# The second plain feed-forward and the unpacking of 4-bit weights, written out as one hand-ordered list

## The chip, the cores and the metric

The kernel runs on one core of one Trainium2 chip, as one program. Its time is the device time of that core in microseconds (us); a result is the median of several executions. The core has five engines with a queue of their own each: TensorE (PE) multiplies matrices, VectorE (DVE) and GpSimd (POOL) do elementwise work, ScalarE (ACT) applies functions such as ReLU, and SyncE (SP) issues transfers. Each engine works through its queue in order. They wait for each other by semaphores.

## The reference

The model has two layers, eight stages in all, over an input `x` of 2 x 1024 tokens with 256 channels in float32. Each stage adds its result to `x`, and each begins with a layer norm. In the order of the computation:

```
x = x + attention_a(layernorm(x))           # layer 0
x = x + ffn0(layernorm(x))
x = x + attention_b(layernorm(x))
x = x + ffn0(layernorm(x))                  # the stage that is changed
x = x + attention_d(layernorm(x))           # layer 1
x = x + ffn1(layernorm(x))
x = x + ttt(layernorm(x))
x = x + ffn1(layernorm(x))
```

Two pieces matter here. The plain feed-forward of layer 0 is

```
h1  = relu(x @ W1.T + b1)      # 256 -> 512
h2  = relu(h1 @ W2.T + b2)     # 512 -> 512
out = h2 @ W3.T + b3           # 512 -> 256
```

and is used twice with the same weights. The feed-forward of layer 1 has three weight matrices (gate, up, down) that come packed: two 4-bit codes to an integer, and one scale for each block of 32 values. A code's low three bits stand for one of 0, 0.5, 1, 1.5, 2, 3, 4, 6, and its fourth bit for the sign. The unpacking turns them into float32 once, ahead of layer 1.

## The kernel before, in words

`x` stays on the chip for the whole program, as 16 tiles of 128 tokens by 256 channels. The function `build` (L1911) runs the stages one after another: the first attention with the first plain feed-forward mixed in, the second attention, `ffn0`, then `dequantize` three times, and after that the stages of layer 1. The attention stages are recorded in an order written out by hand: `in_order` (L277) keeps the order of PE, DVE, ACT and POOL as the code issues it, while SP is left to the framework's scheduler. `ffn0` and `dequantize` are not: there the scheduler orders all engines by its own priorities, and so it mixes the two on its own.

`ffn0` (L637) first makes the layer norm of all 16 tiles, in two halves of eight (`layernorm_T`, L137). DVE takes the statistics (L146, L147), ACT a square root (L148), DVE normalizes (L154), PE turns each tile (L160), and ACT and DVE by turns copy the result out. Then, for each of four groups of 512 tokens, PE multiplies by W1 and W2 (both L654, with a ReLU on ACT at L658) and by W3 (L663). DVE adds the result to `x` (L668), and POOL adds the bias b3 (L669). A float32 product appears in the trace as two records.

`dequantize` (L1325) treats one packed matrix in eight parts of 256 columns, 24 parts in all. For each part SP issues one transfer of codes (L1335) and eight of scales (L1337). DVE makes the magnitude codes `m` and the sign bits `sg` with four masks (L1344, L1345) and the first term `a` (L1352). ACT makes the second term `c` (L1353) and the sign (L1354). POOL adds `c` to `a` (L1355), DVE adds `m` (L1356), POOL multiplies by the sign (L1357), and DVE multiplies by the scales into the weights (L1358). All the tiles of a part have two buffers.

The first plain feed-forward already exists in a second form, `ffn0_pieces` (L403): a list of 22 steps for 512 tokens, which the attention stages lay between their own steps. Its layer norm is by pairs of tiles: `layernorm_stats` (L187), then `layernorm_apply` (L199) with a root in nine small DVE instructions (`rsqrt`, L165) and the normalization on POOL (L205). In this form b3 is added to `x` right after the norm.

Of the kernel before, what the change touches and what calls it, by code (L numbers as in the profile page):

```python
# [39 lines left out]
def interleave_into(out, a, b):  # L40

    interleave([lambda x=x: out.append(x) for x in a], [lambda x=x: out.append(x) for x in b])


class Net:
# [354 lines left out]
            for _, step in mixed(after[2][-held:], chunks[3].outputs):  # L400
                step()

    def ffn0_pieces(self, work, bank, i, w1, w2, w3, b1, b2, b3):  # L403

        nc = self.nc
        f = type("ffn", (), {})()
        f.mv, f.xn = {}, {}

        def stats(p):
            f.mv[p] = self.layernorm_stats(work, (i + 2 * p, i + 2 * p + 1))  # L410

        def rows(p):
            tiles = (i + 2 * p, i + 2 * p + 1)
            f.xn[p] = self.layernorm_apply(work, tiles, f.mv[p], 1, "fxn")
            for tt in tiles:
                xs = self.x[:, tt, :]
                nc.gpsimd.tensor_tensor(xs, xs, b3, ALU.add)

        def turn(p):
            if p == 0:  # L420
                f.xT = work.tile([P, 2, 512], F32, tag="fx", name="fxT", bufs=1)
            pt = bank("ln_t").rearrange("p (k t) -> p k t", k=2)
            for j in range(2):
                for kc in range(2):
                    nc.tensor.transpose(
                        pt[:, kc, j * P : (j + 1) * P], f.xn[p][:, j, kc * P : (kc + 1) * P],
                        self.ident,
                    )
            nc.vector.tensor_scalar_mul(f.xT[:, :, 2 * p * P : 2 * (p + 1) * P], pt, -1.0)

        def hidden(m, part, src, w, bias, dst):
            n = w.shape[1]
            if part == 0:
                f.ph = bank("ph")
                if m == 0:
                    h = work.tile([P, 4, 512], F32, tag=dst, name=dst, bufs=1)
                    setattr(f, dst, h)
            for kc in range(2 * part, 2 * part + 2):
                nc.tensor.matmul(
                    f.ph, w[:, kc, m * P : (m + 1) * P], getattr(f, src)[:, kc],  # L440
                    start=(kc == 0), stop=(kc == n - 1),
                )
            if 2 * part + 2 == n:
                nc.vector.tensor_scalar(
                    getattr(f, dst)[:, m, :], f.ph, bias[:, m : m + 1], 0.0, ALU.add, ALU.max
                )
# [187 lines left out]

    def ffn0(self, w1, w2, w3, b1, b2, b3):  # L637
        nc, tc = self.nc, self.tc
        with ExitStack() as ctx:
            big = ctx.enter_context(tc.tile_pool(name="f_big", bufs=1))  # L640
            work = ctx.enter_context(tc.tile_pool(name="f_work", bufs=2))
            ps = ctx.enter_context(tc.tile_pool(name="f_ps", bufs=2, space=PSUM))
            xT = self.layernorm_T(big, work, ps)
            for c in range(4):
                cols = slice(c * 512, (c + 1) * 512)
                h1 = work.tile([P, 4, 512], F32, tag="h1", name="h1")
                h2 = work.tile([P, 4, 512], F32, tag="h2", name="h2")
                for src, at, n, w, bias, dst in (
                    (xT, cols, 2, w1, b1, h1), (h1, slice(0, 512), 4, w2, b2, h2),
                ):  # L650
                    for m in range(4):
                        ph = ps.tile([P, 512], F32, tag="ph", name="ph", bufs=3)
                        for kc in range(n):
                            nc.tensor.matmul(  # L654
                                ph, w[:, kc, m * P : (m + 1) * P], src[:, kc, at],
                                start=(kc == 0), stop=(kc == n - 1),
                            )
                        nc.scalar.activation(dst[:, m, :], ph, AF.Relu, bias=bias[:, m : m + 1])  # L658
                for j in range(4):
                    tt = 4 * c + j  # L660
                    po = ps.tile([P, C], F32, tag="po", name="po")
                    for kc in range(4):
                        nc.tensor.matmul(  # L663
                            po, h2[:, kc, j * P : (j + 1) * P], w3[:, kc, :],
                            start=(kc == 0), stop=(kc == 3),
                        )
                    xs = self.x[:, tt, :]
                    nc.vector.tensor_tensor(xs, xs, po, ALU.add)  # L668
                    nc.gpsimd.tensor_tensor(xs, xs, b3, ALU.add)  # L669

# [651 lines left out]

    def dequantize(self, pool, name, packed, scales):  # L1325


        nc, tc = self.nc, self.tc
        out = pool.tile([P, 2, 2048], F32, name=name)
        N = 256  # L1330
        with tc.tile_pool(name=f"{name}_dq", bufs=2, side="right") as work:
            for lo in range(0, 2048, N):
                pk = work.tile([P, N], I32, tag="pk", name="pk")
                sc = work.tile([P, N], F32, tag="sc", name="sc")
# [6 lines left out]
                m = work.tile([P, 2, N], I32, tag="m", name="m")  # L1341
                sg = work.tile([P, 2, N], I32, tag="sg", name="sg")
                for dst, mask in ((m, 7), (sg, 8)):
                    nc.vector.tensor_single_scalar(dst[:, 0, :], pk, mask, ALU.bitwise_and)  # L1344
                    nc.vector.tensor_scalar(  # L1345
                        dst[:, 1, :], pk, 4, mask, ALU.logical_shift_right, ALU.bitwise_and
                    )

                a = work.tile([P, 2, N], F32, tag="a", name="a")
                c = work.tile([P, 2, N], F32, tag="c", name="c")  # L1350
                sign = work.tile([P, 2, N], F32, tag="sign", name="sign")
                nc.vector.tensor_scalar(a, m, 4.0, 0.0, ALU.subtract, ALU.max)  # L1352
                nc.scalar.activation(c, m, AF.Relu, bias=self.minus12, scale=2.0)  # L1353
                nc.scalar.activation(sign, sg, AF.Copy, bias=1.0, scale=-0.25)  # L1354
                nc.gpsimd.tensor_tensor(a, a, c, ALU.add)  # L1355
                nc.vector.tensor_tensor(a, a, m, ALU.add)  # L1356
                nc.gpsimd.tensor_tensor(a, a, sign, ALU.mult)  # L1357
                nc.vector.scalar_tensor_tensor(  # L1358
                    out[:, :, lo : lo + N], a, 0.5,
                    sc.unsqueeze(1).to_broadcast([P, 2, N]), ALU.mult, ALU.mult,  # L1360
                )
        return out

    def ffn1_parts(self, ps, work, i, deq):

# [545 lines left out]
def build(tc, ins, out, first=0, last=5):  # L1911
    nc = tc.nc
    with ExitStack() as ctx:
# [12 lines left out]
        with tc.tile_pool(name="w0", bufs=1) as w0:  # L1926
# [14 lines left out]
            for s in todo:  # L1941
                if s == "attn_a":
                    net.attn_a_ffn0(wa, wao, *rope_a, (w1, w2, w3, b1, b2, b3))
                elif s == "ffn0":
                    net.ffn0(w1, w2, w3, b1, b2, b3)
                elif s == "attn_b":
                    net.attn_b(wb, wbo, *rope_b, (w1, w2, w3, b1, b2, b3))
            if {"attn_d", "ttt"} & set(todo):
                w4 = ctx.enter_context(tc.tile_pool(name="w4", bufs=1, side="right"))
                deq = [  # L1950
                    net.dequantize(w4, k, ins[f"L1_ffn_{k}_packed"], ins[f"L1_ffn_{k}_scales"])
                    for k in ("gate", "up", "down")
                ]
        if "attn_d" in todo:
            net.attn_d_ffn1(wd, wdo, *rope_d, nlam, rms_w, deq)
        if "ttt" in todo:
# [103 lines left out]
```

## Time and profile before

The executions took 3041.03 us as the median of three (3031.7 to 3042.51). The profiled execution took 3038.91 us, and its records span 3037.2 us.

| stretch or engine | us |
|---|---|
| span of the profiled execution | 3037.2 |
| PE busy in the span | 2585.5 (85%) |
| DVE busy | 1953.5 (64%) |
| ACT busy | 1324.4 (44%) |
| POOL busy | 1039.6 (34%) |
| last matmul of the second attention ends | 882.0 |
| first statistics of the third attention start | 1041.8 |

Times inside the span count from its start. In rows of the trace, a name such as L654 is the line of the kernel; `h<-ph,b` says that the instruction writes `h` and reads `ph` and `b`; and a note such as `[1.44 <-POOL a L1357]` says how long the engine had been idle before and what ended that. The granted clock is the share of its full rate that TensorE was given.

### The profile page before, as it was taken

How to read it: one execution, taken by the hardware profiler on the slowest of the kernel's cores; microseconds unless marked ns; L12 is line 12 of the kernel's file. 1: busy time of each engine (PE TensorE's matmuls, PEld its weight loads, DVE VectorE, ACT ScalarE, POOL GpSimd, SP SyncE). 2: the span in 40 equal slices, each digit the busy share in tenths (PEclk: the TensorE clock that was granted, in tenths of full speed). 3: DMA queues.
4: the chain of work that ended last, by engine and by line, in shares of the span. 5: the costliest groups of instructions: out<-in, count | busy, mean ns of one | idle time of the engine just before them, and what ended most of it. 6: DMA issues, size and time to landing. Idle time of an engine off the chain costs nothing.

```text
span 3037.2 us, 66929 instructions
## 1 busy us (share of the span) xinstructions
PE 2585.5 (85%) x26384; PEld 1608.0 (53%) x26384; DVE 1953.5 (64%) x6736; ACT 1324.4 (44%) x2672; POOL 1039.6 (34%) x1672
## 2 busy tenths in 40 slices
PE   6999998999988757887878878878777988898988
PEld 2333344434434434565655555555555767677777
DVE  5777665766664456667776858678656656566552
ACT  2776840454453256465564556656622112112110
POOL 3445232212114466566665646556500000000000
PEclk8999997999999867898989888898988889999999
DMA  3000000000001000000000000000001101101100
GB/s 115 1 1 1 1 1 1 1 1 1 1 17 40 28 1 1 1 1 1 1 1 1 1 1 1 1 1 1 18 17 24 24 20 20 23 11 36 24 9 14
DMA packets 61979, 35.39 MB, mean 12 GB/s; under 512 B 43216, under 2 KB 58080, under 8 KB 61664
## 3 DMA queue, kind: packets, MB, share of 16 engines
q1 hardware_dynamic: 59472, 29.49, 3.7%
q8 instruction: 208, 3.41, 0.4%
q10 hardware_dynamic: 2192, 1.61, 0.2%
q14 instruction: 107, 0.88, 0.1%
HBM read 22.68 MB, written 8.39 MB: 10 GB/s over the span
## 4 chain that ended last, share of the span: by engine, by line
PE 38%; DVE 13%; ACT 7%; issue 4%; POOL 3%; DMA 0%; POOLq 0%; ACTq 0%; DVEq 0%
PE ph L1387 6%; PE po L1894 5%; PE pg L1881 4%; ACT p L1200 4%; PE e L1178 4%; DVE p L1189 4%; PE pu L1881 4%; PE dT L1237 3%; PE po L1404 2%; DVE p L1226 2%; POOL p L1213 1%; PE py L1254 1%; PE pq L1564 1%; PE kh L1564 1%; PE pa L1564 1%
## 5 line engine op out<-in xcount | busy, mean ns | idle before, releaser
L1189 DVE CUSTOM_DVE_ANT_0 p<-e,mask 128x512 f32<-128x512 f32 (+3 forms) x768 | 381.6, 553 | 108.9 <-PE e L1178 107.7
L1200 ACT ACTIVATE p<-p,nm 128x128 f32<-128x128 f32 (+7 forms) x512 | 389.9, 764 | 97.4 <-DVE nm L1189 88.1
L1213 POOL TENSOR_SCALAR p<-p,ra,neg_lam 128x128 f32<-128x128 f32 (+7 forms) x256 | 221.8, 866 | 238.1 <-DVE ra L1209 178.6
L1237 PE MATMUL dT<-ident,p 128*128 128x128 f32 x1152 | 198.7, 306 | 114.4 <-ACT pT L1241 32.0
L1241 ACT ACTIVATE pT<-dT 128x128 f32<-128x128 f32 (+7 forms) x256 | 165.4, 646 | 283.5 <-PE dT L1237 282.2
L196 POOL TENSOR_SCALAR ln_mv<-ln_mv 128x2 f32<-128x2 f32 x56 | 17.6, 315 | 730.0 <-DVE ln_mv L194 720.0
L1178 PE MATMUL e<-kT,qT 32*128 32x512 f32 (+3 forms) x1536 | 235.4, 628 | 28.4 <-DVE nm L1189 27.0
L1226 DVE CUSTOM_DVE_ANT_0 p<-p,rs 128x128 f32<-128x128 f32 (+7 forms) x256 | 207.7, 832 | 70.1 <-POOL p L1217 69.8
L1237 PEld LDWEIGHTS dT<-ident,p 128*128 128x128 f32 x1152 | 153.5, 157 | 173.6 <-POOL p L1217 51.4
L845 ACT ACTIVATE pr<-s 128x512 f32<-128x512 f32 (+3 forms) x384 | 157.3, 497 | 162.9 <-PE s L840 154.2
L1230 POOL TENSOR_SCALAR p<-p,md 128x128 f32<-128x128 f32 (+7 forms) x256 | 208.8, 816 | 25.4
L550 ACT ACTIVATE pr<-s 128x1024 f32<-128x1024 f32 (+1 forms) x192 | 145.3, 812 | 131.3 <-PE s L544 83.7
L1894 PE MATMUL po<-down,inter 128*128 128x256 f32 x576 | 164.8, 451 | 3.4 <-issue 2.2
L805 PE MATMUL s<-kT,qT 32*128 32x512 f32 (+3 forms) x768 | 155.3, 518 | 3.8 <-DVE q_pad L813 1.9
L1881 PE MATMUL pg<-xT,gate 128*128 128x256 f32 x576 | 151.5, 409 | 6.5 <-ACT xT L225 5.5
L555 ACT ACTIVATE pr<-pr 128x1024 f32<-128x1024 f32 (+1 forms) x192 | 152.1, 852 | 0.0
L813 DVE CUSTOM_DVE_ANT_0 masked<-s,mask 128x128 f32<-128x128 f32 (+3 forms) x256 | 110.6, 487 | 58.9 <-PE s L805 58.8
L1894 PEld LDWEIGHTS po<-down,inter 128*128 128x128 f32 x576 | 129.8, 230 | 27.8 <-issue 2.3
L558 POOL TENSOR_SCALAR_AFFINE_SELECT pr<-pr 128x256 f32<-128x256 f32 x128 | 90.1, 721 | 154.7 <-ACT pr L555 57.7
L1881 PE MATMUL pu<-xT,up 128*128 128x256 f32 x576 | 139.3, 386 | 0.0
L1887 DVE TENSOR_TENSOR inter<-inter,pu 128x512 f32<-128x512 f32 x72 | 49.3, 685 | 133.9 <-PE pu L1881 133.9
L1387 PE MATMUL ph<-xT,gate 128*128 128x256 f32 x448 | 121.0, 417 | 10.3 <-ACT xT L225 10.1
(313 smaller groups left out, 5398.4 us busy)
## 6 DMA issues: line engine op xcount, KB each, us to landing
uk_d<-uk SPq DMA_DIRECT2D x128, 32.0 KB, 1.9
r<-uk_d SPq DMA_DIRECT2D x8, 512.0 KB, 3.9
x<-in_L_attn_a_X SPq DMA_DIRECT2D x4, 512.0 KB, 6.1
qh_d<-qh SPq DMA_DIRECT2D x8, 256.0 KB, 2.6
o<-qh_d SPq DMA_DIRECT2D x128, 16.0 KB, 1.7
out<-x SPq DMA_DIRECT2D x4, 512.0 KB, 3.1
w<-in_L_ffn_W2T SPq DMA_DIRECT2D x1, 1024.0 KB, 7.8
pk<-in_L_ffn_gate_packed SPq DMA_DIRECT2D x8, 128.0 KB, 2.4
```

The lines of the kernel that those rows point to most:

```text
L845: nc.scalar.activation(pr[:, g, off:512], tiles[g][:, 0:m], AF.Exp, scale=0.25)
L1178: nc.tensor.matmul(own.tiles[h][:, a, 0 : hi - lo], made["q"][r : r + 32, a, t, :], kT[r : r + 32, a, lo:hi], start=True, stop=True,)
L1189: nc.vector.tensor_tensor_reduce(own.p[h][a][:, lo:hi], own.tiles[h][:, a, 0 : hi - lo], neg_row[:, T - nk + lo : T - nk + hi], -1.0, 3e38 ...
L1200: nc.scalar.activation(own.p[h][a], own.p[h][a], AF.Exp, bias=own.nm[:, h, a : a + 1], scale=-1.0, accum_out=own.sm[:, h, a : a + 1],)
L1213: nc.gpsimd.tensor_scalar(p1, p1, own.ra[:, h : h + 1], nlam[:, head : head + 1], ALU.mult, ALU.mult)
L1226: nc.vector.tensor_tensor_reduce(p0, p0, p1, own.rs[:, h, 0:1], -3e38, ALU.add, ALU.max, md)
L1230: nc.gpsimd.tensor_scalar(p0, p0, md, 1.0, ALU.add, ALU.mult)
L1237: nc.tensor.transpose(dT[:, kb, :], own.p[h][0][:, kb * P : (kb + 1) * P], self.ident)
L1241: nc.scalar.activation(pT[:, 0 : qb + 1, :], dT[:, 0 : qb + 1, :], AF.Exp)
L1387: nc.tensor.matmul(ph[:, j, :], w[:, kc, m * P : (m + 1) * P], f.xT[:, kc, :], start=(kc == 0), stop=(kc == 1),)
L1881: nc.tensor.matmul(ph[:, j, :], m_[:, kc, m * P : (m + 1) * P], f.xT[:, kc, :], start=(kc == 0), stop=(kc == 1),)
L1894: nc.tensor.matmul(f.po[:, b], inter[m // 2][:, m % 2, b * P : (b + 1) * P], wd[:, m % 2, (m // 2) * C : (m // 2 + 1) * C], start=(m == 0) ...
```

## The change

The changed kernel drops `ffn0` and replaces it by `ffn0_dequantize`. This makes the 22 steps of `ffn0_pieces` for each of four groups of 512 tokens, and lays the norm of the next group between the later steps of the present one. `dequantize` no longer issues its work; it returns four steps for each of the 24 parts: codes (the transfers), magnitudes (masks, `a`, `c`, sign, and POOL's first add), signs (DVE's add and POOL's multiply), and values (the product with the scales). The steps of neighbouring parts are staggered: in one round stand the values of part n-4, the signs of n-3, the magnitudes of n-2 and the codes of n. The two lists, 88 steps of products and norms and 96 steps of parts, are then laid between each other evenly, and the order on PE, DVE, ACT and POOL is kept as written. A new argument, `scalar`, puts the turned copy and the ReLUs of `ffn0_pieces` on ACT, as the old `ffn0` had its ReLUs, and gives its tiles a second buffer. The buffers of a part grow from two to between two and six. The products, the masks and the arithmetic are the same.

```diff
-            f.xn[p] = self.layernorm_apply(work, tiles, f.mv[p], 1, "fxn")
+            f.xn[p] = self.layernorm_apply(work, tiles, f.mv[p], 1 + scalar, "fxn")
...
-            nc.vector.tensor_scalar_mul(f.xT[:, :, 2 * p * P : 2 * (p + 1) * P], pt, -1.0)
+            xT = f.xT[:, :, 2 * p * P : 2 * (p + 1) * P]
+            if scalar:
+                nc.scalar.activation(xT, pt, AF.Copy, scale=-1.0)
...
+                if scalar:
+                    nc.scalar.activation(out, f.ph, AF.Relu, bias=bias[:, m : m + 1])
...
-    def ffn0(self, w1, w2, w3, b1, b2, b3):
+    def ffn0_dequantize(self, ffn, deq):
...
+            ps = ctx.enter_context(tc.tile_pool(name="f_ps", bufs=1, space=PSUM))
+
+            def bank(name):
+                return ps.tile([P, 512], F32, tag="g", name=name, bufs=8)
+
+            ctx.enter_context(self.in_order())
+            products = []
+            after = [
+                [step for _, step in self.ffn0_pieces(work, bank, 4 * n, *ffn, scalar=True)]
+                for n in range(4)
+            ]
+
+            products += after[0][:6]
+            for n in range(4):
+                products += after[n][6:12]
+                ahead = after[n + 1][:6] if n < 3 else []
+                interleave_into(products, after[n][12:], ahead)
+            unpack = []
+            for args in deq:
+                unpack += self.dequantize(work, *args)
+
+
+            parts = []
+            for n in range(len(unpack) + 4):
+                for m, lag in ((3, 4), (2, 3), (1, 2), (0, 0)):
+                    if 0 <= n - lag < len(unpack):
+                        parts.append(unpack[n - lag][m])
+            interleave(products, parts)
...
+            def codes():
+                pk, sc = tile_("pk", 4, N, dtype=I32), tile_("sc", 6, N)
...
+            def magnitudes():
+
+                pk = t["pk"]
+                m, sg = tile_("m", 3, 2, N, dtype=I32), tile_("sg", 2, 2, N, dtype=I32)
+                a, c, sign = tile_("a", 4, 2, N), tile_("c", 2, 2, N), tile_("sign", 3, 2, N)
...
+            def signs():
+                a = t["a"]
+                nc.vector.tensor_tensor(a, a, t["m"], ALU.add)
+                nc.gpsimd.tensor_tensor(a, a, t["sign"], ALU.mult)
...
+            return codes, magnitudes, signs, values
```

More of the change, by code (lines that the diff above doesn't have):

```diff
@@ L401, in attn_a_ffn0, with ffn0_pieces @@
                 step()
-    def ffn0_pieces(self, work, bank, i, w1, w2, w3, b1, b2, b3):
+    def ffn0_pieces(self, work, bank, i, w1, w2, w3, b1, b2, b3, scalar=False):
         nc = self.nc
@@ L420, in turn @@
             if p == 0:
-                f.xT = work.tile([P, 2, 512], F32, tag="fx", name="fxT", bufs=1)
+                f.xT = work.tile([P, 2, 512], F32, tag="fx", name="fxT", bufs=1 + scalar)
             pt = bank("ln_t").rearrange("p (k t) -> p k t", k=2)
@@ L428, in turn @@
                     )
-            nc.vector.tensor_scalar_mul(f.xT[:, :, 2 * p * P : 2 * (p + 1) * P], pt, -1.0)
+            xT = f.xT[:, :, 2 * p * P : 2 * (p + 1) * P]
+            if scalar:
+                nc.scalar.activation(xT, pt, AF.Copy, scale=-1.0)
+            else:
+                nc.vector.tensor_scalar_mul(xT, pt, -1.0)
         def hidden(m, part, src, w, bias, dst):
@@ L435, in hidden @@
                 if m == 0:
-                    h = work.tile([P, 4, 512], F32, tag=dst, name=dst, bufs=1)
+                    h = work.tile([P, 4, 512], F32, tag=dst, name=dst, bufs=1 + scalar)
                     setattr(f, dst, h)
@@ L443, in hidden @@
             if 2 * part + 2 == n:
-                nc.vector.tensor_scalar(
-                    getattr(f, dst)[:, m, :], f.ph, bias[:, m : m + 1], 0.0, ALU.add, ALU.max
-                )
+                out = getattr(f, dst)[:, m, :]
+                if scalar:
+                    nc.scalar.activation(out, f.ph, AF.Relu, bias=bias[:, m : m + 1])
+                else:
+                    nc.vector.tensor_scalar(
+                        out, f.ph, bias[:, m : m + 1], 0.0, ALU.add, ALU.max
+                    )
         def output(j):
@@ L633, in attn_a_chunk @@
         return chunk
-    def ffn0(self, w1, w2, w3, b1, b2, b3):
+    def ffn0_dequantize(self, ffn, deq):
         nc, tc = self.nc, self.tc
         with ExitStack() as ctx:
-            big = ctx.enter_context(tc.tile_pool(name="f_big", bufs=1))
             work = ctx.enter_context(tc.tile_pool(name="f_work", bufs=2))
[L642 to L669, printed above, removed]
@@ L1321, in attn_d_out, with dequantize, part, tile_ @@
         return squares, root, normalize, project
-    def dequantize(self, pool, name, packed, scales):
-        nc, tc = self.nc, self.tc
-        out = pool.tile([P, 2, 2048], F32, name=name)
+    def dequantize(self, work, out, packed, scales):
+        nc = self.nc
         N = 256
[L1331 to L1334, printed above, removed]
+        def part(lo):
+            t = {}
+            def tile_(name, bufs, *shape, dtype=F32):
+                t[name] = work.tile([P, *shape], dtype, tag=name, name=name, bufs=bufs)
+                return t[name]
+            def codes():
+                pk, sc = tile_("pk", 4, N, dtype=I32), tile_("sc", 6, N)
                 nc.sync.dma_start(pk, packed[:, lo : lo + N])
@@ L1340, in dequantize @@
                     )
-                m = work.tile([P, 2, N], I32, tag="m", name="m")
-                sg = work.tile([P, 2, N], I32, tag="sg", name="sg")
+            def magnitudes():
+                pk = t["pk"]
+                m, sg = tile_("m", 3, 2, N, dtype=I32), tile_("sg", 2, 2, N, dtype=I32)
+                a, c, sign = tile_("a", 4, 2, N), tile_("c", 2, 2, N), tile_("sign", 3, 2, N)
                 for dst, mask in ((m, 7), (sg, 8)):
@@ L1347, in dequantize @@
                     )
-                a = work.tile([P, 2, N], F32, tag="a", name="a")
-                c = work.tile([P, 2, N], F32, tag="c", name="c")
-                sign = work.tile([P, 2, N], F32, tag="sign", name="sign")
                 nc.vector.tensor_scalar(a, m, 4.0, 0.0, ALU.subtract, ALU.max)
@@ L1355, in dequantize, with values @@
                 nc.gpsimd.tensor_tensor(a, a, c, ALU.add)
-                nc.vector.tensor_tensor(a, a, m, ALU.add)
-                nc.gpsimd.tensor_tensor(a, a, sign, ALU.mult)
+            def signs():
+                a = t["a"]
+                nc.vector.tensor_tensor(a, a, t["m"], ALU.add)
+                nc.gpsimd.tensor_tensor(a, a, t["sign"], ALU.mult)
+            def values():
                 nc.vector.scalar_tensor_tensor(
-                    out[:, :, lo : lo + N], a, 0.5,
-                    sc.unsqueeze(1).to_broadcast([P, 2, N]), ALU.mult, ALU.mult,
-                )
-        return out
+                    out[:, :, lo : lo + N], t["a"], 0.5,
+                    t["sc"].unsqueeze(1).to_broadcast([P, 2, N]), ALU.mult, ALU.mult,
+                )
+            return codes, magnitudes, signs, values
+        return [part(lo) for lo in range(0, 2048, N)]
     def ffn1_parts(self, ps, work, i, deq):
@@ L1944, in build @@
                 elif s == "ffn0":
-                    net.ffn0(w1, w2, w3, b1, b2, b3)
+                    w4 = ctx.enter_context(tc.tile_pool(name="w4", bufs=1, side="right"))
+                    names = ("gate", "up", "down")
+                    deq = [w4.tile([P, 2, 2048], F32, name=n) for n in names]
+                    net.ffn0_dequantize((w1, w2, w3, b1, b2, b3), [
+                        (w, ins[f"L1_ffn_{n}_packed"], ins[f"L1_ffn_{n}_scales"])
+                        for n, w in zip(names, deq)
+                    ])
                 elif s == "attn_b":
                     net.attn_b(wb, wbo, *rope_b, (w1, w2, w3, b1, b2, b3))
[L1948 to L1953, printed above, removed]
         if "attn_d" in todo:
```

## The prediction

> **What bounds the kernel now.** The page gives a span of 3037.2 us with TensorE (PE) busy 85%, but that is a mean over stages. The change touches one stage: from the last matmul of the second attention (L872, ends 878.72 + 3.29 = 882.01) to the first statistics of the third attention (L193 at 1041.76), 159.75 us. So I read that stretch alone. First its busy times and granted clock, in windows (columns: window, length, then busy us and instruction count of PE, weight loads, DVE, ACT, POOL, then clock, DMA share, GB/s).
>
> ```profile
> 940.00:950.00 10.00, 8.41 (x16) 3.67 (x17) 4.22 (x13) 4.89 (x8) 5.07 (x4) 0.83 0.20 59
> ...
> 1050.00:1060.00 10.00, 8.30 (x20) 4.48 (x19) 2.52 (x8) 1.41 (x3) 2.36 (x4) 0.50 0.00 0
> ```
>
> ```profile
> 882.00:1042.00 160.00, 128.55 (x353) 68.00 (x352) 89.55 (x239) 53.20 (x87) 72.89 (x66) 0.93 0.13 39
> ```
>
> No engine fills the 160 us. PE's 128.55 is not all work: the 192 recorded passes of L654 follow each other every 0.43 us (26 in 11.43) and the 128 of L663 every 0.215 us (6 in 1.46), so they need 82.6 + 27.5 us; with eight turns of about 0.65 us PE needs 115 us. DVE and POOL are busy 89.55 + 72.89 = 162 us together, which is the length of the stage. Then the list of waits, 904 to 1030 us, where the unpacking of weights (L1335 to L1358) and the products overlap (waiter, releaser, total us, times, longest):
>
> ```profile
> ACT c L1353 <- DVE m L1345: 76.3, 19, 5.9
> ...
> POOL a L1355 <- ACT c L1353: 35.8, 15, 4.6
> DVE a L1356 <- POOL a L1355: 29.7, 21, 1.8
> POOL a L1357 <- DVE a L1356: 16.9, 20, 0.9
> PEld ph L654 <- ACT h L658: 12.5, 7, 3.6
> ...
> PE po L663 <- ACT h L658: 8.7, 5, 4.7
> ```
>
> The engines hand one part of a weight round in a ring: DVE masks, ACT's c, POOL's add, DVE's add, POOL's multiply, DVE's product. Successive parts start 5.4 to 5.5 us apart (L1358 at 917.79, then 923.28). A ReLU (L658) stands in ACT's queue behind c, so PE waits for the ring too. At one place two parts overlap already:
>
> ```profile
> 905.92 0.69 DVE L1356 TENSOR_TENSOR a<-a,m 128x512 f32<-128x512 f32 x1 [0.57 <-POOL a L1355]
> ...
> 906.53 0.28 DVE L1344 TENSOR_SCALAR sg<-pk 128x256 int32<-128x256 int32 x1
> 906.73 0.29 DVE L1345 TENSOR_SCALAR sg<-pk 128x256 int32<-128x256 int32 x1
> 906.75 1.39 POOL L1357 TENSOR_TENSOR a<-a,sign 128x512 f32<-128x512 f32 x1 [0.87 <-DVE a L1356]
> ...
> 906.93 1.50 DVE L1352 TENSOR_SCALAR a<-m 128x512 f32<-128x512 int32 x1
> ...
> 908.35 0.68 DVE L1358 SCALAR_TENSOR_TENSOR gate<-a,sc 128x512 f32<-128x512 f32 x1
> 908.60 1.55 POOL L1355 TENSOR_TENSOR a<-a,c 128x512 f32<-128x512 f32 x1 [0.46 <-DVE a L1352]
> ...
> 910.18 0.69 DVE L1356 TENSOR_TENSOR a<-a,m 128x512 f32<-128x512 f32 x1 [1.16 <-POOL a L1355]
> ```
>
> The reader is to see the durations. L1352 alone takes 0.42; here, beside POOL's L1357, 1.50. POOL's L1355 alone takes 1.26; started during DVE's L1358 it takes 1.55. One excludes the other.
>
> **The change part by part.**
>
> *The ring is pipelined.* In the new list DVE runs, for each part k, the product of part k-2 (V), the add of k-1 (S), then masks and a of k (M); POOL multiplies k-1, then adds c for k. One period, from the start of S: masks at 0.61 and 0.81 (pitch 0.20); POOL's multiply is ready at 0.87 (0.69 + 0.18) and takes the lock at 0.95, ending at 2.21, the lock free at 2.08; masks three and four and a run 2.08 to 2.9; V's lock is 2.85 to 3.38; POOL's add, ready at 3.08, runs 3.38 to 4.65; the next S starts at 4.68. The stretch above is this period with two masks missing: 910.18 - 905.92 = 4.26, plus 2 x 0.20 is 4.66. So 4.68 us a part, against 5.48.
>
> Here a rule speaks against the change. The Trainium skill, "SBUF — State Buffer", section "Who interferes with whom", says that GpSimd and a DVE instruction with two SBUF inputs or in a 2-port mode share one port pair, held for the whole instruction. Whole instructions sum to 4 x 0.285 + 0.42 + 2 x 0.69 + 2 x 1.265 = 5.47 us a part: nothing gained. The rows say less: L1352 ended 0.29 after POOL instead of 0.42, so POOL let go about 0.13 before its recorded end, and L1358 held about 0.53 of its 0.68. I take 4.68, and keep 5.47 as a rival.
>
> *Norms.* Removed: L146 to L160 as one block ahead of everything (16 x 0.54 of L154 on DVE, the Sqrt and its table load of 1.28). Added: eight pairs; each has stats (about 1.05 us, hidden while DVE waits for POOL's add), a root of nine small DVE instructions (1.74 us alone, 3.59 at most beside POOL elsewhere in this trace), and on POOL two L205 (1.09 together) and two bias adds (1.40). POOL's four stand ahead of its next add or multiply, whose DVE and ACT successors wait. Walking the same period with them inserted gives 8.23 for the first pair (root and POOL work together add 3.55) and two periods of 12.9 instead of 9.36 for the second. I charge 3.5 us each, between 1.74 (POOL's share hidden) and 4.23 (root plus 2.49 of POOL, nothing hidden).
>
> *Start.* The first code DMA left at 878.80; in the built order it now also waits for the last L872, so 882.05: codes land 884.5 (2.4 to land) and the second part's 3.9 us later (0.37 + 8 x 0.44 of SP issue), 888.4. DVE's last add ends 882.5; stats and root 885.3; masks of part 0, alternating with POOL's four, 887.5; POOL's add 889.4; S of part 0 at 889.45; the second root with POOL's multiply 892.9; masks of part 1 894.6; POOL free 895.6, its add 896.9. S of part 1 starts at 897.0. PE's first product starts near 895.9; in the old trace half-fed products ran from 891.9 and had by 903.8 done what takes 6.9 us, so this is worth about 1 us, no more.
>
> *ACT.* It now turns all eight pairs (0.6 each, half were DVE's 0.68) and keeps the 32 ReLUs of 0.67: about 58 us, hidden beside 129. With nothing to hide it, 2.4 us.
>
> *SP.* 24 x 3.9 = 94 us, four and six buffers ahead of DVE: hidden. Were it exposed, a part would still cost only 3.9.
>
> *Banks and PE.* Between pieces PE must wait for the second root, queued on DVE behind an add that waits for PE's first output: about 3 us idle, then three outputs. PE has (128 - 115) us of slack, so I charge only the clock: the 940 window shows 0.83 after a 3.6 us wait, 1.7 us lost; half of that on the ring, 0.8 x 3 = 2.4 us.
>
> *End.* Last S at 897.0 + 22 x 4.68 + 6 x 3.5 + 2.4 = 1023.4; multiply and V behind it 2.9 us: 1026.3. The statistics follow directly; the old 0.83 us wait for a bias add goes. The exp table load at 1067.12 (1.28) goes too; L1200's first mean was ready at 1067.99, so 0.4. Gain: 1041.76 - 1026.3 + 0.4 = 15.9, say 16 us. All else stands in the same order.
>
> **Sum.** The profiled execution took 3038.91 us (span 3037.2), so 3023 for its like; against the median of 3041.03 that is 3025 us.
>
> **Rivals.**
>
> *PE becomes the bound:* 0.30 chance. If roots and norms hide in DVE's waits, the stage ends at 895.9 + 115 + 3 = 1014: 28 us gained, 3013. For it: PE's is the longest single sum. Against it: 908.60 and 906.93 above.
>
> *Whole-instruction locking:* 0.17. 22 x 5.47 ends the stage near 1044, so within a few us of before; 3038 to 3044. For it: the skill's rule and the 162 us of DVE and POOL together. Against: the 4.26 measured.
>
> *The clock falls:* 0.06. The row at 1050 has 0.50 with PE busy 8.30 of 10, and the Trainium skill, "TensorE: Matmul & The Clock Gate", section "What's actually happening", gives half rate after an idle window of about 3.4 us; the idle of 3 us between pieces is close. The row at 940 would make each 1.7 us. If instead a share h of the products runs at half rate, PE needs 115(1 + h): it passes the ring at h = 0.13, the old end at 0.27, and is 0.5% slower than before from 0.40 on; at h = 0.5 it ends at 1069, 3068 us.
>
> **How the numbers follow.** The likeliest, the pipelined ring under the lock, has 0.47, centre 3025, own range 3016 to 3034 (period 4.3 to 5.1 over 22 parts). About 0.5%, 15 us, is what can be told from no change: below 3026 is faster. That takes 0.24 of the 0.47 and all 0.30: 0.54; the rest and the locked case: 0.40; the clock: 0.06. The range reaches down past 3013 and up to 3040.
>
> **What would show it.** S to S (the add with m) 4.5 to 4.9 us apart in plain parts and about 8 with a root; DVE's a or masks at 1.2 to 1.5 us beside POOL; third-attention statistics near 1026; granted clock above 0.85 in the stage. It is wrong if periods stay at 5.4, or if PE runs without waits for ACT.

## The result, and the profile after

The changed kernel takes 3040.47 us (median of 20 runs, 3033.15 to 3056.76), the kernel before beside it 3035.89 (20 runs, 3028.07 to 3043.74). The ratio is 1.0013, with a 95% interval of 1.0003 to 1.0023: nothing gained, 4.6 us lost. The forecast of 3025 missed by 15, and by more in what it said of the change: it put 16 us off a median of three runs (3041.03) that twenty runs put 5 us lower, so 16 down was forecast and 4.6 up came, 20.6 apart. The profiled executions say the same of the one stage that changed. From the end of the last projection of the second attention (the last matmul of L881, before L872) to the third attention's statistics (L193) it was 882.01 to 1041.76, 159.75 us; it is 882.89 to 1046.65, 163.8 us. The forecast ended it at 1026.3.

To follow the rows after: masks L1362 and L1363, a L1366, ACT's c L1367 and sign L1368, POOL's add L1369, DVE's add L1373 (S), POOL's multiply L1374, DVE's product L1377 (V), ReLU L451, products of h1 and h2 L444, outputs L460, their add to x L465.

First the windows of the kernel after (window, length, busy us and count of PE, weight loads, DVE, ACT, POOL, then clock, DMA share, GB/s), for the two stretches shown of before:

```profile
882.00:1042.00 160.00, 127.57 (x347) 69.37 (x346) 111.94 (x286) 54.48 (x88) 92.90 (x87) 0.89 0.16 40
...
940.00:950.00 10.00, 10.00 (x25) 4.49 (x24) 6.25 (x15) 4.63 (x8) 4.04 (x3) 1.00 0.11 30
```

DVE and POOL are now busy 205 us in 160, against 162 before, so they do overlap. Some of the rise is time in which one stands locked out by the other (a mask of 0.28 us alone takes 1.36 beside POOL's multiply, rows below). PE fills the ten microseconds from 940 completely. It does so only in the h1 and h2 products; over the stage its clock is 0.89 against 0.93.

Then the waits of the kernel after, 904 to 1030 us (waiter, releaser, total us, times, longest), to lay beside those of before:

```profile
ACT h L451 <- PE ph L444: 35.1, 18, 4.3
ACT c L1367 <- DVE m L1363: 25.6, 9, 3.8
DVE a L1373 <- POOL a L1369: 23.7, 8, 5.4
POOL a L1369 <- ACT c L1367: 17.9, 5, 5.4
...
PE po L460 <- ACT h L451: 9.6, 3, 3.2
```

New at the top is ACT waiting for PE: 35 us in which the ReLU at the head of ACT's queue has no product yet. Below it POOL's add waits for c, and DVE's S for that add. Before, 76 us of ACT waiting for DVE's masks stood at the top.

The place where this happens, in order of time (start, us, engine, line, operation, tiles, idle time before it and its releaser):

```profile
939.46 0.68 DVE L1373 TENSOR_TENSOR a<-a,m 128x512 f32<-128x512 f32 x1
...
940.26 0.28 DVE L1363 TENSOR_SCALAR m<-pk 128x256 int32<-128x256 int32 x1
940.28 1.39 POOL L1374 TENSOR_TENSOR a<-a,sign 128x512 f32<-128x512 f32 x1 [1.29 <-DVE a L1373]
...
940.56 0.69 ACT L451 ACTIVATE h<-ph,b 128x512 f32<-128x512 f32 x1 [3.41 <-PE ph L444]
...
942.28 0.69 ACT L451 ACTIVATE h<-ph,b 128x512 f32<-128x512 f32 x1 [1.03 <-PE ph L444]
...
944.00 0.69 ACT L451 ACTIVATE h<-ph,b 128x512 f32<-128x512 f32 x1 [1.03 <-PE ph L444]
...
944.58 0.71 ACT L1367 ACTIVATE c<-m,minus 128x512 f32<-128x512 int32 x1
...
945.37 1.27 POOL L1369 TENSOR_TENSOR a<-a,c 128x512 f32<-128x512 f32 x1 [3.70 <-ACT c L1367]
...
946.67 0.69 DVE L1373 TENSOR_TENSOR a<-a,m 128x512 f32<-128x512 f32 x1 [3.72 <-POOL a L1369]
```

The second of the two masks that c needs is done at 940.54. In the list, c stands behind the third ReLU of h1. PE delivers one h1 product every 1.72 us, so ACT comes to c only at 944.58, four microseconds later. POOL's add and S wait for it: this period is 7.21 us. Nothing else held it, for a was ready at 942.35. The profile puts seven of POOL's waits in the stage down to c. This is one; the others are:

```profile
906.45 1.27 POOL L1369 TENSOR_TENSOR a<-a,c 128x512 f32<-128x512 f32 x1 [5.41 <-ACT c L1367]
983.82 1.28 POOL L1369 TENSOR_TENSOR a<-a,c 128x512 f32<-128x512 f32 x1 [2.98 <-ACT c L1367]
1023.51 1.28 POOL L1369 TENSOR_TENSOR a<-a,c 128x512 f32<-128x512 f32 x1 [4.23 <-ACT c L1367]
1028.66 1.27 POOL L1369 TENSOR_TENSOR a<-a,c 128x512 f32<-128x512 f32 x1 [1.62 <-ACT c L1367]
1035.53 1.27 POOL L1369 TENSOR_TENSOR a<-a,c 128x512 f32<-128x512 f32 x1 [3.33 <-ACT c L1367]
1041.03 1.27 POOL L1369 TENSOR_TENSOR a<-a,c 128x512 f32<-128x512 f32 x1 [2.10 <-ACT c L1367]
```

The one at 945.37 and the first three here are the same place of each of the four pieces, the h1 products. At the next two c stands behind ReLUs of the last piece's h2. These six are 21.3 us. At the last, 1041.03, c waits for its masks, which stand on DVE behind an output's add to x that PE has not served yet.

Three more waits, 4.9 us in all, are put down to DVE's statistics in the profile's list, but end like the others 0.08 us after a c that stands behind a ReLU without a product:

```profile
910.22 0.69 ACT L451 ACTIVATE h<-ph,b 128x512 f32<-128x512 f32 x1 [2.75 <-PE ph L444]
...
910.81 0.71 ACT L1367 ACTIVATE c<-m,minus 128x512 f32<-128x512 int32 x1
...
911.60 1.27 POOL L1369 TENSOR_TENSOR a<-a,c 128x512 f32<-128x512 f32 x1 [1.62 <-DVE ln_st L193]
```

Its masks were done at 908.84, and POOL's add does not read the statistics. So nine times, 26.1 us in all, POOL waited for a c behind ReLUs.

The other direction, at the end of the first piece's h2 products:

```profile
922.73 0.72 ACT L1367 ACTIVATE c<-m,minus 128x512 f32<-128x512 int32 x1 [3.80 <-DVE m L1363]
924.14 0.63 ACT L1368 ACTIVATE sign<-sg 128x512 f32<-128x512 int32 x1 [0.69 <-DVE sg L1363]
...
924.68 0.67 ACT L451 ACTIVATE h<-ph,b 128x512 f32<-128x512 f32 x1
...
925.40 5.84 PE L460 MATMUL po<-w,h 128*128 128x256 f32 x18 [3.18 <-ACT h L451]
```

The last product of h2 ends at 920.48 in the trace. Its ReLU stands behind c and sign of a part, which wait for DVE's masks, and these for POOL; it starts at 924.68. PE idles 3.2 us here, and then the first eight passes follow each other every 0.43 us instead of 0.22. So each of the two strands waits for the other in turn, through ACT's queue. I read from this that the stage comes to the slower of the two in each stretch, added up, which is more than either strand's own sum; the two strands by themselves, below, allow an estimate of it.

### The profile page after: what moved, and what is told of

Its sections match the earlier page's. It is cut to its first block, busy times and chain, and to the rows that moved or that the text cites. A ratio compares the mean times of both kernels' runs of the same rounds, so it can differ in the third digit from the quotient of the medians.

```text
span 3039.6 us, 66932 instructions
## 1 busy us (share of the span) xinstructions
PE 2582.3 (85%) x26384; PEld 1607.1 (53%) x26384; DVE 1977.6 (65%) x6786; ACT 1325.3 (44%) x2672; POOL 1062.2 (35%) x1696
## 4 chain that ended last, share of the span: by engine, by line
PE 59%; DVE 19%; ACT 8%; issue 5%; POOL 5%; DMA 0%; SPq 0%; POOLq 0%; DVEq 0%; ACTq 0%
PE ph L1409 5%; PE po L1916 5%; PE pg L1903 4%; DVE p L1198 4%; PE ph L444 4%; PE e L1187 4%; PE pu L1903 4%; ACT p L1209 4%; PE s L814 4%; PE dT L1246 3%; PE s L849 2%; PE py L868 2%; PE s L553 2%; POOL p L1222 2%; DVE p L1235 2%
## 5 line engine op out<-in xcount | busy, mean ns | idle before, releaser
L854 ACT ACTIVATE pr<-s 128x512 f32<-128x512 f32 (+3 forms) x384 | 157.3, 496 | 162.8 <-PE s L849 154.2
L1409 PE MATMUL ph<-xT,gate 128*128 128x256 f32 x448 | 119.8, 414 | 10.4 <-ACT xT L225 10.1
```

The lines of the kernel that those rows point to most:

```text
L1409: nc.tensor.matmul(ph[:, j, :], w[:, kc, m * P : (m + 1) * P], f.xT[:, kc, :], start=(kc == 0), stop=(kc == 1),)
```

## The experiments

Theory 1: the ring's pace and the norms are as the prediction had them; the list deals the steps by count, and ring and products stop each other through the in-order queues, ACT's first. Theory 2: the lock between DVE and POOL is the bound, and the ring alone is no faster. Theory 3: PE's own losses, half clock after each idle and the norms between pieces, are the bound. All stage lengths below are from one profile each, measured as above; against before, the stage moved by +4.0, -2.4, -10.1, -14.6 and -15.9 us in the five kernels that were also timed (the changed one, by time, add later, one root, one root by time), and the medians by +4.6, -0.3, -13.0, -17.5 and -21.3.

**The ring without products.** The list of steps stays, products are replaced by nothing; the feed-forward is not computed.

```diff
-            interleave(products, parts)
+            norms = [s for a in after for s in a[:6]]
+            interleave([s if s in norms else (lambda: None) for s in products], parts)
```

> The changed list with the products of the feed-forward left out (the matmuls of h1, h2 and the outputs, their ReLUs and the adds of the outputs to x), everything else at its place: so the feed-forward is not computed, while norms, turns and all unpacking run. Theory 1 (the ring's own pace under the lock is what the walk said, 4.68 us a part and 3.5 us for each pair of norms, and in the changed kernel it stands still behind the products, and they behind it): the adds with m start 4.5 to 4.9 us apart in plain parts, about 8.2 with a root, and from the second to the last of the 24 it is 115 to 128 us, against 144.3 in the changed kernel. Theory 2 (DVE and POOL are the bound: with whole instructions excluding each other the ring needs 5.47 us a part by itself): 140 us or more, plain parts 5.4 apart.

From the second S to the last it is 125.85 us, and the stage 144.7. In the changed kernel the same path is 144.29, from 898.81 to 1043.11. DVE's rows of this kernel (lines are one higher: S is L1374, masks L1363 and L1364, a L1367, V L1378):

```profile
898.99 0.69 DVE L1374 TENSOR_TENSOR a<-a,m 128x512 f32<-128x512 f32 x1 [2.96 <-POOL a L1370]
899.60 0.29 DVE L1363 TENSOR_SCALAR m<-pk 128x256 int32<-128x256 int32 x1
...
900.00 1.36 DVE L1363 TENSOR_SCALAR sg<-pk 128x256 int32<-128x256 int32 x1
...
901.82 0.68 DVE L1378 SCALAR_TENSOR_TENSOR gate<-a,sc 128x512 f32<-128x512 f32 x1
903.65 0.69 DVE L1374 TENSOR_TENSOR a<-a,m 128x512 f32<-128x512 f32 x1 [1.15 <-POOL a L1370]
...
1024.84 0.69 DVE L1374 TENSOR_TENSOR a<-a,m 128x512 f32<-128x512 f32 x1 [1.15 <-POOL a L1370]
```

The period is 4.66 us with the masks of one part beside POOL's multiply (1.36 instead of 0.28 for the one that is locked out), just as in the prediction, and the periods with the first root of a piece are 8.20. Theory 2 is out.

Set against the changed kernel part by part, the periods of the four h1 places above are 8.94 against 4.66, 7.21 against 4.65, 6.51 against 4.65 and 7.76 against 4.74. They make 11.7 of the 18.4 us between the two paths. The four periods that follow them, where c stands behind a ReLU of h2, add 2.9, and the last two of the path 3.8. The periods with adds of outputs to x add 2.5: these adds stand on DVE and are left out here. Against this, 2.45 us go the other way: one period of the ring alone is 8.70 and not 6.25, because set-up of the next stage (L975 to L995) comes to stand among POOL's work there (1000.81 to 1004.85). In the changed kernel this set-up comes after the last part.

**The products without the ring.**

```diff
-            interleave(products, parts)
+            for w, packed, _ in deq:
+                for half in range(2):
+                    nc.sync.dma_start(w[:, half, :], packed.bitcast(F32))
+            interleave(products, [])
```

> The changed list with the unpacking left out: the three weights are filled by plain loads of the packed codes, so their values are meaningless, while the feed-forward and its norms run as in the list. From the end of the last projection of the second attention to the third attention's statistics: theory 1 (each of the two, products and ring, is well below the sum of their waits on each other): 125 to 135 us (115 us of matmuls, about 8 ahead of the first one with norms of 4 us each and small stalls between pieces), against 163.7 in the changed kernel. Theory 3 (the clock's loss after each idle and the norms between pieces keep the products themselves from being faster): 145 us or more.

The stage is 126.5 us. PE's row of windows of this kernel:

```profile
878.00:1004.00 126.00, 118.12 (x352) 65.07 (x352) 27.89 (x121) 26.43 (x40) 21.23 (x42) 0.96 0.11 45
```

PE is busy 118 of 126 us at a clock of 0.96. Theory 3 is out: norms between pieces and the start cost PE little when no ring is in the way. So the two strands need 144.7 and 126.5 us by themselves, and 163.8 together.

An estimate for one piece, from the eighth S of the changed kernel (939.46) to the fourteenth (978.62): beside h1 and h2, PE's 48 passes at 0.43 us need 20.6, and the three parts there take 17.6 in the ring alone. Beside outputs and turns, the next three parts take 17.3 in the ring alone, and PE needs some 8 (32 passes at 0.215, two turns of 0.65). The slower in each stretch makes 20.6 + 17.3 = 37.9; measured are 39.2, of which 0.9 go to the adds to x. The ring's own sum is 34.9, PE's 29.

**Steps dealt out by time.**

```diff
-            interleave(products, parts)
+            pe = ring = 0.0
+            for k, step in enumerate(products):
+                step()
...
+                ring += 3.5 * (step in norms)
+                pe += 1.72 * (step in long)
+                while parts and ring + parts[0][0] / 2 <= 1.2 * pe:
+                    us, part = parts.pop(0)
+                    ring += us
+                    part()
```

> The same products in the same order and the same unpacking, but the steps of the unpacking are dealt out by time (1.72 us for each step of products, 4.7 for a part, 3.5 for each pair of norms) and not by count, so that more parts stand beside the h1 and h2 products and fewer beside outputs and norms. Theory 1: the adds with m inside h1 and h2 come about 4.7 apart, the waits of outputs for ReLUs and of ring for c become small, and the stage is 8 to 14 us shorter than in the changed kernel (150 to 156 us), the whole 3026 to 3033. Theory 2 (lock) and theory 3 (clock): within 3 us of the changed kernel.

The stage is 157.3 us, 6.4 shorter than in the changed kernel, a little less than expected; the whole is 3035.73, ratio to before 0.9998 (0.9986 to 1.0010). Thirteen of its periods are 4.66 to 4.68, as expected, but three are 11.3 to 11.7, which was not. Its waits, 904 to 1030 us:

```profile
PE ln_t L426 <- POOL ln_xn L205: 13.1, 7, 4.3
DVE x L465 <- PE po L460: 12.3, 3, 4.3
...
POOL a L1384 <- ACT c L1382: 8.6, 3, 3.9
```

Three waits for c are left. The other loop is through DVE, here at the first of the three long periods:

```profile
933.86 3.05 PE L460 MATMUL po<-w,h 128*128 128x256 f32 x8
...
936.95 0.42 DVE L465 TENSOR_TENSOR x<-x,po 128x256 f32<-128x256 f32 x1 [3.85 <-PE po L460]
937.29 0.69 DVE L1388 TENSOR_TENSOR a<-a,m 128x512 f32<-128x512 f32 x1
```

An output's add to x stands ahead of S on DVE, the output stands behind a turn on PE, the turn waits for POOL's normalized rows, and these for the root on DVE. This deal moved waits more than it removed them.

**POOL's add one part later.** M stays one step of the list, without POOL's add; that comes a part later, with one more buffer for each tile that lives longer. The dealing by count stays, but the list has 24 steps more, and against the products M comes to stand two or three steps earlier: that of the ninth part before the first h1 product of its piece, not behind the third (worked out from the two lists).

```diff
-                nc.gpsimd.tensor_tensor(a, a, c, ALU.add)
+            def adds():
+                nc.gpsimd.tensor_tensor(t["a"], t["a"], t["c"], ALU.add)
...
-            for n in range(len(unpack) + 4):
-                for m, lag in ((3, 4), (2, 3), (1, 2), (0, 0)):
+            for n in range(len(unpack) + 5):
+                for m, lag in ((4, 5), (3, 4), (1, 2), (2, 3), (0, 0)):
```

> POOL's addition of c is a step of its own, one part later in the list, with one more buffer for m, sg, a, c, sign and sc; nothing else. So a c that stands behind a ReLU has a whole period before anyone waits for it. Theory 1 in its narrow form (c late behind ReLUs holds the ring): the waits of POOL's add for c go from 17.9 us in sum to below 5, and the stage is 5 to 10 us shorter than in the changed kernel, after some 3 us for the longer drain. Theory 2 (lock) or theory 3 (clock): 0 to 4 us longer, by the drain.

The stage is 149.7 us, 14.1 shorter than in the changed kernel, more than expected, and the whole is 3023.06 (15 runs), ratio to before 0.9959 (0.9947 to 0.9970). Its waits, 904 to 1030 us (POOL's add is L1371, its multiply L1376):

```profile
POOL a L1376 <- DVE a L1375: 27.9, 15, 5.6
...
PEld ph L444 <- ACT h L451: 2.5, 5, 1.5
POOL a L1371 <- ACT c L1367: 1.9, 1, 1.9
```

POOL's waits for c fell from 17.9 us to 1.9, and those of the outputs on PE for a ReLU are gone. Is it the room or M's new place? At that h1 place c is not late any more, so the place has its share. But as in the changed kernel, c starts late (0.9 to 6.8 us after its masks) directly behind a ReLU in nine parts, in part the same and in part others, and only once does POOL wait. For example:

```profile
1016.23 0.28 DVE L1363 TENSOR_SCALAR m<-pk 128x256 int32<-128x256 int32 x1
...
1019.27 0.69 ACT L451 ACTIVATE h<-ph,b 128x512 f32<-128x512 f32 x1 [2.75 <-PE ph L444]
...
1019.86 0.71 ACT L1367 ACTIVATE c<-m,minus 128x512 f32<-128x512 int32 x1
...
1022.09 1.31 POOL L1371 TENSOR_TENSOR a<-a,c 128x512 f32<-128x512 f32 x1
```

This c is 3.35 us late, not much less than that of 944.58 in the changed kernel (4.04), and POOL's add needs it only 1.5 us after its end. The waits show the room at work; the 14.1 us are not split between the two. What POOL waits for now is DVE, which is busy 126.1 of the 151 us:

```profile
885.00:1036.00 151.00, 125.80 (x355) 68.38 (x354) 126.09 (x292) 54.15 (x88) 94.17 (x94) 0.91 0.17 42
```

**Control: the ring of that kernel without products** (the first experiment's edit on it; the feed-forward is not computed).

> The list with POOL's addition of c one part later, and the products of the feed-forward left out as before (matmuls of h1, h2 and outputs, ReLUs, the adds of outputs to x), so the feed-forward is not computed. Control for what the later addition does to the ring by itself. If the gain of 14 us with the later addition came from c no longer standing in the way: the ring by itself gains little, S of the second to S of the last part 121 to 126 us (125.8 with the addition in its old place), plain parts 4.5. If the later addition made the ring itself faster and the products never mattered: 110 to 115 us.

122.74 us from the second S to the last, plain parts 4.48, the stage 142.8. So the later add makes the ring itself only 3.1 us faster on that path (125.85 to 122.74), and takes 12.1 of the 18.4 us that the products had put on it: 144.29 less 125.85 is 18.4, 129.06 less 122.74 is 6.3. (Set-up of the next stage stands among POOL's work in this run too, and lengthens one period by 1.3 us, against 2.45 in the other; without it the later add takes 13.3 of 20.9.) Of the 6.3 nearly all lies in two periods, 8.27 against 6.12 and 8.29 against 4.49, where S stands on DVE behind an output's add to x that waits for PE, 1.71 and 3.39 us. The second:

```profile
1027.87 0.42 DVE L465 TENSOR_TENSOR x<-x,po 128x256 f32<-128x256 f32 x1 [3.39 <-PE po L460]
1028.21 0.68 DVE L1375 TENSOR_TENSOR a<-a,m 128x512 f32<-128x512 f32 x1
```

**The overlap undone.** M, S and V of a part follow each other in one round of the list, with products between them as before.

```diff
-                for m, lag in ((3, 4), (2, 3), (1, 2), (0, 0)):
+                for m, lag in ((1, 2), (2, 2), (3, 2), (0, 0)):
```

> The changed list with the ring's overlap undone: masks, the add with m, the multiplication and the product of one part follow each other in one step, as the kernel before handed a part round, while products, norms and the places of the steps stay. If the overlap works and its gain was given back by waits on the products: S of the second to S of the last part 150 to 170 us against 144.3 in the changed kernel, the stage 170 to 185. If the overlap never gave anything in this list, because the products pace it: within 3 us of 144.3.

147.6 us from the second S to the last, the stage 168.5. The expectation for "its gain was given back" missed on both counts, if narrowly; the other, within 3 us, missed too, by 0.3. Plain parts are 5.43 us apart, the pace of the kernel before (941.95, then 947.38), and parts with a root 8.89, so overlap is worth 0.77 us a part where nothing stands in the way; over 22 periods that would be 17 us. Only 3.3 us of it show on that path and 4.8 in the stage. From the sixth S to the twelfth, one whole piece, the rows say why. Without overlap it is 39.8 us, and four times 5.43 with twice 8.89 is 39.5, so this slower ring hardly ever waits for a product. With overlap the ring alone takes 34.9, and the changed kernel 38.5: of the 4.9 us gained by overlap 3.6 are spent waiting for products. The stage can now be told as a sum: before 159.75; the new list without overlap 168.5, 8.8 more; overlap, 4.8 less, 163.8.

**One root for pieces 2 to 4,** on the kernel with the later add.

```diff
+            def root():
+                nc.gpsimd.tensor_scalar(mv[:, :, 0], mv[:, :, 0], -1.0, 1.0, ALU.mult, ALU.mult)
+                roots["y"] = self.rsqrt(work, mv[:, :, 1], 1.0, 1e-5, "lna")
...
-                products += after[n][6:12]
-                ahead = after[n + 1][:6] if n < 3 else []
+                begin = [lambda k=k: stats(k) for k in range(0, 12, 2)] + [root] if n == 0 else []
+                interleave_into(products, after[n][6:12], begin)
+                ahead = []
+                if n < 3:
+                    ahead = [
+                        lambda n=n: rows(n + 1, 0), after[n + 1][3],
+                        lambda n=n: rows(n + 1, 1), after[n + 1][5],
+                    ]
```

> The later addition, and the norms of pieces 2 to 4 with one root for all twelve tiles, their statistics dealt out over the first piece's products, instead of six roots of nine small instructions each between the parts. In the kernel with the later addition DVE has no gap left in plain parts and each pair of norms adds about 4 us to the ring. If DVE is the bound there: 5 roots of 1.74 us go, and each root's stall of POOL behind it: the stage is 6 to 12 us shorter than with the later addition alone (138 to 144 us), the whole 3012 to 3018. If products or POOL bound it: within 3 us.

The stage is 145.2 us, 4.5 shorter and less than the 6 to 12 expected. The whole is 3018.88 (11 runs), ratio 0.9948 (0.9933 to 0.9963), an interval that overlaps that of the later add alone, so the step between the two rests on the stage in the profiles. The profiled execution itself, 3030.44 us, is no guide to the whole: its stage began 10.6 us later than that of the kernel before the change, behind work that was not edited.

**The same, dealt out by time** (the loop above, with 4.5 us for a part, 2.5 for a pair of norms and 1.12).

> As the run before, and the steps dealt out by time (1.72 us for a step of products, 4.5 for a part, 2.5 for a pair of norms, 1.12 us of ring for each us of products), so that the last adds of outputs to x no longer stand ahead of the ring's last parts on DVE (3.4 us of waits there with the later addition). If alternation of ring and products still costs at the pieces' ends: 2 to 6 us shorter than the run before; if the ring alone is the bound: within 2 us of it.

The stage is 143.8 us, 1.4 shorter, so within the 2 us of "the ring alone is the bound". The whole is 3015.07 (4 runs), ratio 0.9941 (0.9924 to 0.9959): the fastest median of these kernels, 25 us under the changed one, though not to be told from the run before it. Its windows:

```profile
880.00:1025.00 145.00, 122.24 (x355) 65.07 (x353) 115.30 (x248) 54.77 (x88) 91.61 (x89) 0.94 0.18 44
```

PE is busy 122 and DVE 115 of 145 us, so both still stand idle for over 20. That the ring is the bound here is not shown: no run has the ring of this kernel by itself.

## Why the prediction was wrong

*The ring is pipelined: right by itself.* 4.68 us a part was forecast, 4.66 measured without products, 4.66 to 4.68 in the kernel dealt out by time, and 4.94 at best in the changed kernel. The rule weighed there (a lock for the whole instruction, 5.47) is contradicted by these numbers, as by the 4.26 of before.

*Norms: right.* 3.5 us for a pair; without products the first pair of a piece adds 8.20 less 4.66, 3.54, the second 6.35 plus 6.26 less twice 4.66, 3.29.

*Start: nearly.* The second S was put 14.95 us after the end of the attention and came at 15.9; PE's first product 13.85 after it and came at 14.7, at half rate for its first four passes (0.85 to 1.01 us instead of 0.43).

*SP: right.* DVE's waits for the DMAs of codes and scales sum to 0.2 us.

*End: right in itself.* 2.9 us behind the last S were forecast, 3.5 came.

*Sum of the ring.* From the second S to the last the prediction had 22 x 4.68 + 21 + 2.4 = 126.4 us. The ring without products takes 125.85 and its stage 144.7, against the 144.3 of the forecast. That this is so close is in part luck: the 2.4 us were charged for the clock after PE's waits, which that run does not have, while it has 2.45 us of set-up on POOL that the forecast did not have. Without both it is 124.0 against 123.4, still right. With products the path takes 144.29. These 17.9 us, with 0.9 at the start and 0.6 at the end, are the whole miss of the stage. Some 2.5 of them lie in the periods with adds of outputs to x on DVE, a term that the sum had left out.

*ACT, "about 58 us, hidden beside 129": the step that failed.* The sum is right (54.5 busy) and the conclusion false. A queue in order hides nothing if what stands at its head waits for another engine: nine times POOL waited 1.6 to 5.4 us for a c that stood behind ReLUs without a product, 26.1 us in all. The prediction had read the other half of this in the profile of before ("stands in ACT's queue behind c, so PE waits for the ring too") and did not turn it round. The later add, which gives c room before POOL needs it and moves M up by two or three products, gives back 12.1 of the 18.4 us that the products cost the ring.

*Banks and PE, "PE has (128 - 115) us of slack, so I charge only the clock": failed with it.* The slack is a mean over the piece. In the h1 and h2 products PE has none (48 passes at 0.43 us without a gap, and a full window), and the ring waits for it there. At outputs, turns and norms the ring has none, and PE waits. PE's idle between pieces was not one wait of 3 us but two, 3.6 us before the output passes that need the last block of h2, and 2.5 to 4.1 before the turns, from pass to pass.

*Rivals.* PE as the bound did not come: with products alone the stage is 126.5. Whole-instruction locking was given 3038 to 3044, and the result lies there, but by another way, since the ring keeps 4.66; a time that fits a rival does not make its mechanism. The clock did lose at each piece's end (0.89 over the stage for 0.93), which I read as a consequence of the waits and not their cause: it is 0.96 with the products alone, and where many of the waits went, it came back to 0.94. What no rival named was that ring and products could add up in part. Of the stated signs, the statistics came at 1046.65 and not near 1026, and no period lies between 4.5 and 4.9; DVE's long masks, the roots' 8.2 and a clock above 0.85 came. But the stated way to be wrong, "if periods stay at 5.4, or if PE runs without waits for ACT", does not cover two strands that each wait for the other.

Two things stay open. In the changed kernel itself, what goes from c to the ring and what from ReLU to PE is not separated, since both run through the same queue; nor, in the later add, the room from M's new place. And 8.8 us more in the list without overlap than before are not split between norms moved into the ring and the order itself.

## What to carry to other kernels

When two strands of work are written as one list over in-order queues, add up each stretch of the list, not the whole: the time tends to the sum over stretches of the slower strand, unless one strand may run ahead of the list. For each instruction at the head of a shared queue ask what it waits for and who stands behind it, in both directions. Here, each against the list it changed, room to run ahead (one more buffer and the consumer one part later, which also moved M up) bought 14 us of the stage, dealing the steps out by time bought 6, and making the strand itself faster had bought 5.

## What the runs showed of the hardware

With the later add DVE has no gap left in plain parts, and two masks of a part, not one, are locked out, once by POOL's multiply (941.15 to 942.54) and once by its add behind it (1.31 us). In the kernel with the later add (S is L1375, V L1379):

```profile
941.13 0.28 DVE L1363 TENSOR_SCALAR m<-pk 128x256 int32<-128x256 int32 x1
941.33 1.36 DVE L1362 TENSOR_SCALAR sg<-pk 128x256 int32<-128x256 int32 x1
942.61 1.35 DVE L1363 TENSOR_SCALAR sg<-pk 128x256 int32<-128x256 int32 x1
943.88 0.41 DVE L1366 TENSOR_SCALAR a<-m 128x512 f32<-128x512 int32 x1
```

So the period is 4.49 and no longer a chain through POOL: it is DVE's own time, 0.6 + 0.2 + 0.2 + 1.28 + 1.27 + 0.34 + 0.6 from start to start, of which 2.1 us is standing still. In these parts more overlap has nothing left to fill; fewer masks on DVE would be the next thing to try, which no run here did. I had not expected that a single later add would move the bound of the ring from POOL's chain to DVE.
